# Local attention in a decoder: the output projection of one sequence-layer in one block of 256 tokens instead of two blocks of 128

## Chip, core and metric

The kernel runs on one core of one Trainium2 chip. The metric is the device time of one execution in microseconds (us). The engines of the core work side by side: TensorE (PE for its matmuls, PEld for its weight loads), VectorE (DVE), ScalarE (ACT), GpSimd (POOL) and SyncE (SP), which here only issues DMAs. Each works through its own instructions in order and waits on semaphores of the others.

## What is computed

A decoder of three parts over 8 sequences of 256 tokens with 128 features, all in float32: a state-space block, a cross-attention block and six layers of local attention with a feed-forward. The change lies in the local attention, whose layer the reference writes like this:

```python
def attn_layer(x, Wqkv, qs, ksc, Wo):
    q, k, v = jnp.split(x @ Wqkv, 3, -1)
    sh = lambda t: t.reshape(b, n, HEADS, DIM_HEAD).transpose(0, 2, 1, 3)
    q, k, v = (sh(q), sh(k), sh(v))
    q = l2norm(q) * qs
    k = l2norm(k) * ksc
    ...
    out = local_attention(q, k, v)      # windows of 32, each sees itself and the one before
    out = out.transpose(0, 2, 1, 3).reshape(b, n, INNER)
    return out @ Wo                     # INNER = 16 heads * 64 = 1024, back to 128
for i in range(DEPTH):                  # 6
    x = attn_layer(shift_tokens(x), ...) + x
    x = ffn_layer(shift_tokens(x), ...) + x
```

The last product, `out @ Wo`, and the sum with `x` behind it are what the change touches.

## The kernel before, in words

The first two parts (state-space, cross-attention) end at about 715 us of the profile and are not touched. The third part handles 48 sequence-layers (6 layers of 8 sequences) one after the other. The work is not left to a scheduler on TensorE and VectorE: inside `tc.manual_schedule` their instructions stand in the order in which the program issues them. That order is the list `slots` (lines 1174 to 1201). `run(n)` goes through it once for each sequence-layer n; I call this a **pass**. A slot `(f, k, ...)` does step `f` for sequence-layer n + k, so that one pass works on three neighbouring sequence-layers. A blank line divides the list into four groups, the **tiles** 1 to 4 of a pass. On TensorE they hold:

- tiles 1 and 3: `value` (v_ps, line 875), `scores` (s_ps, line 979), `turn` of the queries (qkT_ps, line 931), a piece of a feed-forward, `turn_weights` (pT_ps, line 1021), `query_key` (qk_ps, line 875);
- tiles 2 and 4: `project_out` (y_ps, line 1052), `attend` (o_ps, line 1038), `turn` of the keys (qkT_ps, line 931), a piece of a feed-forward, `turn_weights`, `query_key`.

The other engines in this part:

- VectorE: for each tile the two rotary products of `query_key` (lines 892 and 893, they read qk_ps), the sums of squares (ss, line 905), maximum and sum of the weights (mx, lines 1000, 1012, 1013). In tiles 1 and 3 also twice `masked` (line 991, reads s_ps), in tiles 2 and 4 also the sum `x + y_ps` of `project_out` (line 1060) and two 32x32-block transposes of o_ps into oT (line 1046).
- ScalarE: the squares of qk_ps (sq, line 898), the copies out of qkT_ps (lines 938 for queries, 941 for keys), of v_ps (918) and pT_ps (1025), roots and exponentials (line 98).
- GpSimd: 896 (rotary sum), 1001 and 1014 (weights), 924 (`normalise`: queries or keys times their inverse length).

Keys that tile 2 turns were normalised in tile 1 of the same pass, one tile before. Those that tile 4 turns, and all queries, were normalised two tiles before or more.

A feed-forward serves a pair of sequences, in pieces spread over two passes by the slots `("ff",)`. In the passes of odd n, tile 2 holds its variance (ln_var, line 1106), behind which ScalarE makes the inverse root (ln_sq, line 98) and VectorE the normalised input (fxn, line 1108), and tile 3 holds its first products (f_ps, line 1122). In the passes of even n the rest follows (lines 1122, 1128, 1150, 1151).

PSUM is handed out from two-buffer pools: "big" tiles of two banks hold qk_ps, v_ps, qkT_ps and two thirds of f_ps; "s" tiles of one bank hold y_ps, pT_ps, ln_var and the like. A matmul into a big tile waits until what was there has been read.

`project_out(n, wh)` (lines 1048 to 1065) does one half of a sequence: eight matmuls accumulate the 1024 inner features in eight blocks of 128, with the weights `Wo` as the stationary operand and 128 tokens of oT as the moving one. In the trace each float32 matmul is two records, so one half is 16 records with 16 weight loads. The half with wh = 0 of sequence-layer n - 1 stands in tile 2 of pass n, the half with wh = 1 in tile 4. `attend(n, 0)` and `attend(n, 1)` fill oT for them: attend(n, 0) in tile 4 of pass n, attend(n, 1) in tile 2 of pass n + 1.

Of the kernel before, what the change touches and what calls it, by code (L numbers as in the profile page):

```python
# [9 lines left out]
FP = mybir.dt.float32  # L10
# [4 lines left out]
P = 128  # L15
# [8 lines left out]
H, HD = 16, 64  # L24
# [25 lines left out]
def decoder_kernel(ctx: ExitStack, tc: tile.TileContext, a: dict, out: bass.AP):  # L50
    nc = tc.nc
    V, A, G, T = nc.vector, nc.scalar, nc.gpsimd, nc.tensor
# [12 lines left out]
    def ps_s(name):  # L65
        return banks[-1].tile([P, 512], FP, tag="s", name=name)
# [4 lines left out]
    def ps_two(name):  # L71

        return banks[-1].tile([P, 2, 512], FP, tag="two", name=name, bufs=1)
# [121 lines left out]
    def new_x(p):  # L195
        return xp.tile([P, TP], FP, tag=f"x{p}", name=f"x{p}")
# [104 lines left out]
    with (  # L301
# [450 lines left out]
        for p in range(NPAIR):  # L752
# [3 lines left out]
            for n in range(NS):  # L756
                state(p, c, n)
                if n == 0:
# [3 lines left out]
                    for h in range(2):  # L762
                        t = ps1.tile([P, TP], FP, tag=f"xm{h}", name="xm_ps", bufs=1)
# [33 lines left out]
    x2 = [None] * NPAIR  # L797
    pools3, fixed3, x3, done = {}, {}, [], set()
    wts, thirds, tabs = {}, {}, {}
# [46 lines left out]
    def batch(xs, b):  # L846
        return xs[b // 2][:, (b % 2) * S : (b % 2 + 1) * S]

    seq = [(d, b) for d in range(DEPTH) for b in range(B)]
    tiles3 = [(wh, g) for wh in range(2) for g in range(2)]  # L850

    got = [{} for _ in seq]

    def shift(n):

        d, b = seq[n]
        if d + 1 < DEPTH:
            if b == 3:
                load(d + 1)
                load_table3(d + 1)  # L860
            if b == 6:
                load_third(d + 1, 0)
        x = batch(x2 if d == 0 else x3, b)
        xs = pools3["a"].tile([P, S], FP, name="xs", bufs=3)
        G.memset(xs[HD:, 0:1], 0.0)
        A.copy(xs[:HD, :], x[:HD, :])
        A.copy(xs[HD:, 1:], x[HD:, : S - 1])
        got[n]["xs"] = xs
        got[n]["ss"] = pools3["a"].tile([P, 4, H], FP, name="ss", bufs=3)
        got[n]["rn"] = pools3["a"].tile([P, 4, H], FP, name="rn", bufs=3)  # L870
# [157 lines left out]
    def attend(n, wh):  # L1028

        o_ps = ps_two("o3_ps")  # L1030
        for g in range(2):
            pT, vz = got[n]["pT", 2 * wh + g], got[n]["vz", 2 * wh + g]
            for j in range(4):
                for i in range(4):
                    for e in range(2):
                        r = slice(e * HD, (e + 1) * HD)
                        c = (4 * g + j) * HD
                        T.matmul(  # L1038
                            o_ps[i * W : (i + 1) * W, e, c : c + HD],
                            lhsT=pT[r, j, i * W : (i + 1) * W], rhs=vz[r, j, i, :],  # L1040
                            start=True, stop=True, tile_position=(e * HD, i * W),
                        )

        oT = got[n]["oT", wh] = pools3["b"].tile([P, 2, 2, 4 * HD], FP, name="oT3")
        for g in range(2):
            V.transpose(oT[:, g], o_ps[:, :, g * 256 : (g + 1) * 256])  # L1046

    def project_out(n, wh):
        d, b = seq[n]
        y_ps = ps_s("y3_ps")  # L1050
        for hb in range(NHB):
            T.matmul(  # L1052
                y_ps[:, :P], lhsT=wts[d][0][:, hb, :],
                rhs=got[n]["oT", wh][:, hb // 4, (hb // 2) % 2, :].rearrange(
                    "p (w h q) -> p h w q", w=4, h=2
                )[:, hb % 2],
                start=(hb == 0), stop=(hb == NHB - 1),
            )
        half = slice(wh * P, (wh + 1) * P)
        V.tensor_tensor(  # L1060
            batch(x3, b)[:, half], batch(x2 if d == 0 else x3, b)[:, half], y_ps[:, :P],
            ALU.add,
        )
        if wh:
            got[n].clear()

    def feed_forward(d, p, b=None):
# [86 lines left out]
    def finish(p, b=None):  # L1154

        at = slice(0, TP) if b is None else slice(b * S, (b + 1) * S)
        x = x3[p][:, at]
        m = at.stop - at.start
        V.tensor_tensor(x, x, x2[p][:, at], ALU.add)
        yield from layernorm_steps(x, x)  # L1160
        yield
        tp = ps_s("st_ps")[:, :m]
        for j in range(m // P):
            T.transpose(tp[:, j * P : (j + 1) * P], x[:, j * P : (j + 1) * P], ident)
        ot = pools3["w"].tile([P, INNER], FP, tag="wqkv", name="st_o", bufs=4)[:, :m]
        A.copy(ot, tp)
        o = out[2 * p : 2 * p + 2] if b is None else out[2 * p + b : 2 * p + b + 1]
        nc.sync.dma_start(
            out=o.rearrange("b (c q) d -> q (b c) d", q=P),
            in_=ot.rearrange("q (c d) -> q c d", d=D),  # L1170
        )
        yield
# [4 lines left out]
    q, k = 0, 1  # L1177
# [4 lines left out]
        (peak, 0, 2), ("end", 1), ("ff",), (turn_weights, 0, 0), (add_weights, 0, 1),  # L1182
        (query_key, 1, k, 1), (root, 1, k, 0), (normalise, 1, k, 0),

        ("end", 1), (weigh, 0, 2), (place, 0, 2), (project_out, -1, 0),
        (attend, -1, 1), (squares, 1, k, 1), (turn, 1, k, 0),
        (peak, 0, 3), ("end", 0), ("ff",), (turn_weights, 0, 1), (add_weights, 0, 2),
        (query_key, 2, q, 0), (root, 1, k, 1), (normalise, 1, k, 1), (shift, 3),
# [3 lines left out]
        (peak, 1, 0), ("end", 1), ("ff",), (turn_weights, 0, 2), (add_weights, 0, 3),  # L1192
        (root, 2, q, 0), ("late",), (query_key, 2, q, 1), (normalise, 2, q, 0),

        (weigh, 1, 0), (place, 1, 0), (project_out, -1, 1),
        (attend, 0, 0), (squares, 2, q, 1), (turn, 1, k, 1),
        (peak, 1, 1), ("end", 0), ("end", 1), ("ff",), (turn_weights, 0, 3), (add_weights, 1, 0),
        (query_key, 2, k, 0), (root, 2, q, 1), (normalise, 2, q, 1),
# [4 lines left out]
    def ends():  # L1203

        while True:
            while queue and next(queue[0], queue) is queue:
                queue.pop(0)
            yield

    end = ends()  # L1210

    def run(n):
        nonlocal ff
        for f, *args in slots:
            k, *args = args or [0]
            if f == "ff" or (f == "late" and n % 2):
                next(ff, None)
            elif f == "late":
                pass
            elif f == "end":  # L1220
                if k != n % 2:
                    next(end)
            elif 0 <= n + k < len(seq) and (f, n + k, *args) not in done:
                f(n + k, *args)
                if f is project_out and args[0]:
                    d, b = seq[n + k]
                    last = d == DEPTH - 1
                    if b % 2:
                        ff = feed_forward(d, b // 2)
                        next(ff)  # L1230
                    elif last and b == B - 2:
                        queue.extend((feed_forward(d, b // 2, 0), finish(b // 2, 0)))
                    if last and b % 2 and b > 1:
                        queue.append(finish(b // 2 - 1))
# [27 lines left out]
    with tc.tile_pool(name="s2", bufs=2, reuse_waits="tile") as sp:  # L1262
# [52 lines left out]
        for p in range(NPAIR):  # L1315
# [6 lines left out]
            oT = sp.tile([P, NHB, TP], FP, name="oT2", bufs=1)  # L1322
# [9 lines left out]
            y_ps = ps_s("y2_ps")  # L1332
            for hb in range(NHB):
                T.matmul(
                    y_ps, lhsT=w2["wo"][:, hb, :], rhs=oT[:, hb, :], start=(hb == 0), stop=(hb == NHB - 1)
# [11 lines left out]
    with ExitStack() as st:  # L1347
        cp = st.enter_context(tc.tile_pool(name="s3c", bufs=1, reuse_waits="tile"))
        pools3["b"] = st.enter_context(tc.tile_pool(name="s3", bufs=2, reuse_waits="tile"))
        fixed3["mask"] = cp.tile([P, NW, 2 * W], FP, name="mask")  # L1350
        nc.sync.dma_start(out=fixed3["mask"], in_=a["c_mask"])


        fixed3["kz"] = cp.tile([P, NHB, W + S], FP, name="kz")
        fixed3["vzs"] = [cp.tile([P, 4, 4, HD], FP, name=f"vz{i}") for i in range(6)]
        for t in [fixed3["kz"]] + fixed3["vzs"]:
            G.memset(t, 0.0)
        x3.extend(new_x(p) for p in range(NPAIR))

        with tc.manual_schedule(engines={mybir.EngineType.PE, mybir.EngineType.DVE}):  # L1360
            shift(1)
            for n in range(-1, len(seq)):
                run(n)
            project_out(len(seq) - 1, 0)
            attend(len(seq) - 1, 1)
            for _ in ff:
                pass
            next(end)
            project_out(len(seq) - 1, 1)
            tail = feed_forward(DEPTH - 1, NPAIR - 1, 1)  # L1370
            queue.append(finish(NPAIR - 2))
            while queue:
                next(tail, None)
                next(end)
            for _ in tail:
                pass
            for _ in finish(NPAIR - 1, 1):
                pass
# [86 lines left out]
```

## Time and profile before

| | us |
|---|---|
| three timed runs | 2239.37, 2244.81, 2244.76 |
| their median | 2244.76 |
| span of the profiled execution, first to last instruction | 2235.6 |
| PE busy in it | 2096.8 (94%) |
| DVE busy | 1743.8 (78%) |
| POOL busy | 1636.2 (73%) |
| ACT busy | 1422.2 (64%) |

The span of the profiled execution leaves out what lies before its first and after its last instruction; the three timed runs are 3.8 to 9.2 us longer. Of the groups of instructions, the projection's are among the costlier ones on TensorE: 1536 matmul records of line 1052 with 187.5 us of busy time, and as many weight loads.

A row of the timeline gives the start of a group, the time from its start to its end, engine, line, operation, the tile written and the tiles read, the number of instructions, and in brackets how long the engine stood idle before it and what ended that. Records of TensorE overlap: the end of a group is later than the start of the next one.

### The profile page before, as it was taken

To read this page: it belongs to the slowest core of one execution; us is meant where nothing else is said; L and a number is where in the kernel's file an instruction comes from. 1 tells how busy PE (TensorE), PEld (TensorE's weight loads), DVE (VectorE), ACT (ScalarE), POOL (GpSimd) and SP (SyncE) were. 2 spreads that over 40 slices of the span, in tenths; PEclk is the share of its full clock that TensorE was granted. 3 is DMA by queue.
4 is the path that set the end of the run, shared out by engine and by line. 5 is a ranking of instruction groups with operands and counts; after the bars stand their busy time and mean duration, and the time that the engine had idled before them with its cause. 6 is when DMAs were issued, how large, how long until landed. Compare 5 with 4: busy or idle time off the path is not lost.

```text
span 2235.6 us, 77068 instructions
## 1 busy us (share of the span) xinstructions
PE 2096.8 (94%) x32482; PEld 1314.8 (59%) x32482; DVE 1743.8 (78%) x2533; ACT 1422.2 (64%) x2432; POOL 1636.2 (73%) x1440
## 2 busy tenths in 40 slices
PE   7787879999998999999999999999999999999986
PEld 3232334444445766666767767676767767676663
DVE  5988986353467988888888888888888888888762
ACT  4544546455556776777767677777767677777554
POOL 3988985132268988888888888888888888888750
PEclk8888889999999999999999999999999999999998
DMA  4434431000204444334443434343443434333330
GB/s 124 119 104 100 105 102 31 1 5 1 83 7 68 71 71 95 67 71 75 74 88 71 79 65 94 68 79 67 75 88 69 78 67 84 68 65 64 65 62 10
DMA packets 438326, 155.41 MB, mean 70 GB/s; under 512 B 401886, under 2 KB 418140, under 8 KB 437852
## 3 DMA queue, kind: packets, MB, share of 16 engines
q1 hardware_dynamic: 437500, 150.10, 34.2%
q8 instruction: 255, 4.18, 0.8%
q14 instruction: 91, 0.75, 0.1%
q10 hardware_dynamic: 480, 0.38, 0.1%
HBM read 54.68 MB, written 1.31 MB: 25 GB/s over the span
## 4 chain that ended last, share of the span: by engine, by line
PE 73%; DVE 13%; ACT 7%; issue 4%; POOL 3%; DMA 0%; SPq 0%; DVEq 0%; POOLq 0%; ACTq 0%
PE qk_ps L875 13%; PE y_ps L1052 8%; PE qkT_ps L931 7%; PE o_ps L1038 7%; PE f_ps L1122 6%; PE v_ps L875 6%; PE s_ps L979 5%; DVE m L691 4%; PE pT_ps L1021 3%; PE f_ps L1150 3%; PE o_ps L1296 2%; PE pr L279 2%; PE s_ps L1277 2%; DVE wz L721 2%; ACT ln_sq L98 1%
## 5 line engine op out<-in xcount | busy, mean ns | idle before, releaser
L896 POOL TENSOR_TENSOR qk<-qk,rb 128x512 f32<-128x512 f32 x384 | 481.0, 1275 | 49.0 <-DVE rb L893 30.6
L924 POOL TENSOR_TENSOR qk<-qk,rn 128x1024 f32<-128x1024 f32 x192 | 365.5, 1904 | 12.8 <-ACT rn L98 12.8
L875 PE MATMUL qk_ps<-wqkv,xs 128*128 128x512 f32 x768 | 363.3, 595 | 2.4 <-ACT kz L941 1.4
L1001 POOL TENSOR_TENSOR pw<-pw,mx 128x512 f32<-128x512 f32 x192 | 202.1, 1052 | 164.6 <-DVE mx L1000 164.3
L898 ACT ACTIVATE sq<-qk_ps 128x1024 f32<-128x1024 f32 x192 | 197.0, 1026 | 165.8 <-PE o_ps L1038 122.6
L892 DVE TENSOR_TENSOR qk<-qk_ps,tab 128x1024 f32<-128x1024 f32 x192 | 228.9, 1192 | 66.6 <-PE qk_ps L875 65.1
L905 DVE TENSOR_REDUCE ss<-sq 128x16 f32<-128x1024 f32 x192 | 229.4, 1195 | 6.2 <-ACT sq L898 6.1
L893 DVE TENSOR_TENSOR rb<-qk_ps,tab 128x1024 f32<-128x1024 f32 x192 | 233.3, 1215 | 0.0
L1014 POOL TENSOR_TENSOR pw<-pw,mx 128x512 f32<-128x512 f32 x192 | 200.4, 1044 | 39.1 <-ACT fxn L1109 32.0
L1286 POOL TENSOR_TENSOR ws<-w 128x512 f32<-128x512 f32 x64 | 81.4, 1272 | 196.8 <-ACT w L98 154.1
L1052 PEld LDWEIGHTS y_ps<-oT,wo 128*128 128x128 f32 x1536 | 186.2, 192 | 46.6 <-issue 33.5
L931 PE MATMUL qkT_ps<-ident,qk 128*128 128x128 f32 x1536 | 210.6, 280 | 2.9 <-POOL qk L924 2.9
L1052 PE MATMUL y_ps<-oT,wo 128*128 128x128 f32 x1536 | 187.5, 275 | 1.9 <-ACT pT L1025 1.6
L1046 DVE STREAM_TRANSPOSE oT<-o_ps 128x512 f32<-128x512 f32 x192 | 126.1, 695 | 80.9 <-PE o_ps L1038 80.9
L875 PEld LDWEIGHTS qk_ps<-wqkv,xs 128*128 128x128 f32 x768 | 131.2, 191 | 97.2 <-issue 92.7
L979 PEld LDWEIGHTS s_ps<-kz,qT 64*32 64x32 f32 x12288 | 138.2, 105 | 74.5 <-issue 33.4
L875 PE MATMUL v_ps<-wqkv,xs 128*128 128x512 f32 x384 | 180.5, 592 | 0.3 <-ACT sq L898 0.3
L931 PEld LDWEIGHTS qkT_ps<-ident,qk 128*128 128x128 f32 x1536 | 165.9, 141 | 23.0 <-POOL qk L924 3.8
L98 ACT ACTIVATE ab<-dt,aa 128x512 f32<-128x512 f32 x128 | 87.6, 689 | 143.1 <-DVE m L691 142.9
L726 POOL TENSOR_TENSOR dw<-wz 128x512 f32<-128x512 f32 x128 | 133.9, 1046 | 56.1 <-DVE wz L721 56.1
L691 DVE TENSOR_TENSOR_SCAN m<-dw,ab 128x256 f32<-128x256 f32 x256 | 160.9, 669 | 12.8 <-POOL mc L693 11.4
L1038 PE MATMUL o_ps<-vz,pT 64*32 64x64 f32 x12288 | 168.0, 225 | 1.7 <-issue 1.7
(217 smaller groups left out, 4178.7 us busy)
## 6 DMA issues: line engine op xcount, KB each, us to landing
vz<-v SPq DMA_DIRECT2D x1152, 64.0 KB, 2.2
rows<-bc_dram SPq DMA_DIRECT2D x126, 256.0 KB, 3.9
vz<-v SPq DMA_DIRECT2D x576, 32.0 KB, 2.1
wqkv<-in_L_ffn_Wqkv SPq DMA_DIRECT2D x18, 512.0 KB, 4.4
wo<-in_L_ffn_Wo SPq DMA_DIRECT2D x48, 64.0 KB, 2.6
w<-in_L_ffn_W SPq DMA_DIRECT2D x6, 341.0 KB, 3.1
t_in<-in_x SPq DMA_DIRECT2D x4, 256.0 KB, 3.4
wkv<-in_L_xattn_Wkv SPq DMA_DIRECT2D x1, 1024.0 KB, 7.9
```

The source lines that it names most:

```text
L691: V.tensor_tensor_scan(m[:, t], i["dw"][:, t], i["ab"][:, t], 0.0, ALU.add, ALU.mult)
L875: T.matmul(pr[:, i * 512 : (i + 1) * 512], lhsT=got[n]["xs"][:, tb * P : (tb + 1) * P], rhs=thirds[seq[n][0], c][:, i * 512 : (i + 1) * 51 ...
L892: V.tensor_tensor(t, p3, cs, ALU.mult)
L893: V.tensor_tensor(rb, p3, sn, ALU.mult)
L896: G.tensor_tensor(t[:, :, o], t[:, :, o], rb[:, :, f], ALU.add)
L905: V.tensor_reduce(got[n]["ss"][:, 2 * c + tb, :], got[n]["sq"], AX.X, ALU.add)
L924: G.tensor_tensor(t, t, r, ALU.mult)
L931: T.transpose(t_ps[:, hb * P : (hb + 1) * P], t[:, 2 * hb : 2 * hb + 2, :].rearrange("p h d -> p (h d)"), ident,)
L979: T.matmul(s_ps[i * W : (i + 1) * W, e, c : c + 2 * W], lhsT=qT[r, 4 * g + i, j * W : (j + 1) * W], rhs=kz[r, 4 * g + i, k0 : k0 + 2 * W], ...
L1001: G.tensor_tensor(pw, pw, mx[:, 0].unsqueeze(3).to_broadcast([P, 4, 2, 2 * W]), ALU.subtract)
L1038: T.matmul(o_ps[i * W : (i + 1) * W, e, c : c + HD], lhsT=pT[r, j, i * W : (i + 1) * W], rhs=vz[r, j, i, :], start=True, stop=True, tile_p ...
L1052: T.matmul(y_ps[:, :P], lhsT=wts[d][0][:, hb, :], rhs=got[n]["oT", wh][:, hb // 4, (hb // 2) % 2, :].rearrange("p (w h q) -> p h w q", w=4 ...
```

## The change

Both halves are projected at once, in tile 4, and nothing is projected in tile 2. For this oT of both halves is one tile (of one buffer, twice as large as each of the two before); the matmuls take 256 tokens each, eight instead of two times eight for a sequence-layer; one sum of 256 columns takes the place of two of 128. The last sequence-layer keeps its two halves.

```diff
-        oT = got[n]["oT", wh] = pools3["b"].tile([P, 2, 2, 4 * HD], FP, name="oT3")
+        if "oT" not in got[n]:
+            got[n]["oT"] = pools3["b"].tile([P, 2, 2, 2, 4 * HD], FP, name="oT3", bufs=1)
         for g in range(2):
-            V.transpose(oT[:, g], o_ps[:, :, g * 256 : (g + 1) * 256])
+            V.transpose(got[n]["oT"][:, wh, g], o_ps[:, :, g * 256 : (g + 1) * 256])

-    def project_out(n, wh):
+    def project_out(n, whs=(0, 1)):
         d, b = seq[n]
+        m = len(whs) * P
         y_ps = ps_s("y3_ps")
+        oT = got[n]["oT"][:, whs[0] : whs[-1] + 1]
         for hb in range(NHB):
             T.matmul(
-                y_ps[:, :P], lhsT=wts[d][0][:, hb, :],
-                rhs=got[n]["oT", wh][:, hb // 4, (hb // 2) % 2, :].rearrange(
-                    "p (w h q) -> p h w q", w=4, h=2
-                )[:, hb % 2],
+                y_ps[:, :m], lhsT=wts[d][0][:, hb, :],
+                rhs=oT[:, :, hb // 4, (hb // 2) % 2, :].rearrange(
+                    "p t (w h q) -> p t h w q", w=4, h=2
+                )[:, :, hb % 2],
                 start=(hb == 0), stop=(hb == NHB - 1),
             )
...
-        ("end", 1), (weigh, 0, 2), (place, 0, 2), (project_out, -1, 0),
+        ("end", 1), (weigh, 0, 2), (place, 0, 2),
         (attend, -1, 1), (squares, 1, k, 1), (turn, 1, k, 0),
...
-        (weigh, 1, 0), (place, 1, 0), (project_out, -1, 1),
+        (weigh, 1, 0), (place, 1, 0), (project_out, -1),
         (attend, 0, 0), (squares, 2, q, 1), (turn, 1, k, 1),
...
-            project_out(len(seq) - 1, 0)
+            project_out(len(seq) - 1, (0,))
             attend(len(seq) - 1, 1)
...
-            project_out(len(seq) - 1, 1)
+            project_out(len(seq) - 1, (1,))
```

In the built programs the orders of ScalarE, GpSimd and SyncE are the same before and after; on TensorE and VectorE only the projection's own instructions move.

More of the change, by code (lines that the diff above doesn't have):

```diff
@@ L1042, in attend @@
                         )
-        oT = got[n]["oT", wh] = pools3["b"].tile([P, 2, 2, 4 * HD], FP, name="oT3")
+        if "oT" not in got[n]:
+            got[n]["oT"] = pools3["b"].tile([P, 2, 2, 2, 4 * HD], FP, name="oT3", bufs=1)
         for g in range(2):
-            V.transpose(oT[:, g], o_ps[:, :, g * 256 : (g + 1) * 256])
-    def project_out(n, wh):
+            V.transpose(got[n]["oT"][:, wh, g], o_ps[:, :, g * 256 : (g + 1) * 256])
+    def project_out(n, whs=(0, 1)):
         d, b = seq[n]
+        m = len(whs) * P
         y_ps = ps_s("y3_ps")
+        oT = got[n]["oT"][:, whs[0] : whs[-1] + 1]
         for hb in range(NHB):
             T.matmul(
-                y_ps[:, :P], lhsT=wts[d][0][:, hb, :],
-                rhs=got[n]["oT", wh][:, hb // 4, (hb // 2) % 2, :].rearrange(
-                    "p (w h q) -> p h w q", w=4, h=2
-                )[:, hb % 2],
+                y_ps[:, :m], lhsT=wts[d][0][:, hb, :],
+                rhs=oT[:, :, hb // 4, (hb // 2) % 2, :].rearrange(
+                    "p t (w h q) -> p t h w q", w=4, h=2
+                )[:, :, hb % 2],
                 start=(hb == 0), stop=(hb == NHB - 1),
             )
-        half = slice(wh * P, (wh + 1) * P)
+        half = slice(whs[0] * P, whs[0] * P + m)
         V.tensor_tensor(
-            batch(x3, b)[:, half], batch(x2 if d == 0 else x3, b)[:, half], y_ps[:, :P],
+            batch(x3, b)[:, half], batch(x2 if d == 0 else x3, b)[:, half], y_ps[:, :m],
             ALU.add,
         )
-        if wh:
+        if whs[-1]:
             got[n].clear()
@@ L1224, in run @@
                 f(n + k, *args)
-                if f is project_out and args[0]:
+                if f is project_out:
                     d, b = seq[n + k]
```

## Prediction

> **What bounds the kernel now.** I read the page first, then the table of waits between 760 and 2180 us, then the timeline of one odd and one even pass. On the page:
>
> ```profile
> PE 2096.8 (94%) x32482; PEld 1314.8 (59%) x32482; DVE 1743.8 (78%) x2533; ACT 1422.2 (64%) x2432; POOL 1636.2 (73%) x1440
> ...
> PE 73%; DVE 13%; ACT 7%; issue 4%; POOL 3%; DMA 0%; SPq 0%; DVEq 0%; POOLq 0%; ACTq 0%
> ```
>
> TensorE is busy 94% of the span and 73% of the chain that ended last. But an average does not say what happens where work is taken out. The table of waits does (engine and line that waited, releaser, total us, times, longest):
>
> ```profile
> DVE oT L1046 <- PE o_ps L1038: 78.0, 91, 1.7
> ...
> PE f_ps L1122 <- ACT sq L898: 13.8, 22, 0.8
> ...
> DVE fxn L1108 <- ACT ln_sq L98: 12.0, 22, 0.7
> ```
>
> TensorE has one wait that comes back: 22 times, some 0.63 us each, once in every odd pass with a feed-forward, at f_ps in tile 3. At that point the others are late, not TensorE. The timeline of pass 23 shows what they are late with (tile 2 begins at 1407.01, tile 3 at 1414.54, tile 4 at 1424.57):
>
> ```profile
> 1407.01 1.95 PE L1052 MATMUL y_ps<-oT,wo 128*128 128x128 f32 x16
> ...
> 1407.68 1.90 POOL L924 TENSOR_TENSOR qk<-qk,rn 128x1024 f32<-128x1024 f32 x1
> ...
> 1408.77 1.21 DVE L893 TENSOR_TENSOR rb<-qk_ps,tab 128x1024 f32<-128x1024 f32 x1
> 1408.88 1.78 PE L1038 MATMUL o_ps<-vz,pT 64*32 64x64 f32 x128
> ...
> 1410.08 1.03 ACT L898 ACTIVATE sq<-qk_ps 128x1024 f32<-128x1024 f32 x1 [1.69 <-DVE rb L893]
> 1410.60 1.09 PE L931 MATMUL qkT_ps<-ident,qk 128*128 128x128 f32 x8
> ...
> 1410.89 1.31 DVE L1046 STREAM_TRANSPOSE oT<-o_ps 128x512 f32<-128x512 f32 x2 [0.72 <-PE o_ps L1038]
> ...
> 1411.72 1.01 ACT L941 COPY kz<-qkT_ps 128x1024 f32<-128x1024 f32 x1 [0.62 <-PE qkT_ps L931]
> ...
> 1414.37 1.21 DVE L1108 SCALAR_TENSOR_TENSOR fxn<-ln_xc,cols,ln_sq 128x512 f32<-128x512 f32 x1 [0.46 <-ACT ln_sq L98]
> ...
> 1418.66 1.02 ACT L898 ACTIVATE sq<-qk_ps 128x1024 f32<-128x1024 f32 x1 [0.44 <-DVE rb L893]
> ...
> 1419.74 2.84 PE L1122 MATMUL f_ps<-fxn,w 128*128 128x512 f32 x6 [0.78 <-ACT sq L898]
> ```
>
> f_ps needs the big PSUM tile that holds qk_ps of tile 2, free once ScalarE has squared it (1418.66 to 1419.68). That square waits for VectorE, which goes without a gap from fxn at 1414.37 over mx, the reciprocal and the rotary products. **So between the removed block and the added one stands a point that VectorE and ScalarE set.**
>
> **The change, part by part.**
>
> The price of a block. From one record's start to the next: y_ps (1.95 - 0.275)/15 = 0.112 us, 0.275 being the mean record of line 1052 on the page. For 256 columns this even pass has a row with the same weights' size:
>
> ```profile
> 1444.76 1.46 PE L1150 MATMUL f_ps<-fh,w 128*128 128x256 f32 x6
> ```
>
> (1.46 - 0.38)/5 = 0.216 us, 0.38 being the mean record of that group. Sixteen records of 128 columns take 1.79 us, sixteen of 256 take 3.46. So tile 2 loses 1.79, tile 4 gains 3.46 - 1.79 = 1.67, and TensorE's own work shrinks by 0.12 us a pass, 47 x 0.12 = 5.6 us in all. Eight weight loads of 192 ns go too, but they lie beside the matmuls and set nothing. The new operand is read in pieces of 32 columns, as the old one was; from the side of the rows, a record could cost between half of qk_ps's 512 columns (in pass 23 four records last 1.88, one 0.595 on the page: (1.88 - 0.595)/3 = 0.428, half of it 0.214) and twice the old one (0.223), which is no saving at all. I take 0.216, a row of just this width.
>
> A page has this differently. By the Trainium skill ("TensorE: Matmul & The Clock Gate", section "Back-to-back issue gap") a stream of pairs of weight load and matmul was measured at about 81 ns a matmul for 128 columns and 131 ns for 512, which makes width nearly free. An estimate from it for 256 columns is 98 ns, the saving then 32 x 81 - 16 x 98 ns = 1.0 us a pass, some 48 us for 47 passes. The rows above (0.112, 0.216, 0.429 us) follow the columns; I go by them.
>
> VectorE: two sums of 0.28 us become one of 256 columns; the nearest row, ln_xc of line 1102 with 128x256, has 0.41. In tile 4 it ends before o_ps is ready, for which VectorE waits there anyway (0.94 us in pass 23), so it is free; in tile 2 0.19 us of VectorE go. If that cover were gone, it would cost 0.13 us a pass. The single buffer of oT adds no wait: attend's transposes in tile 4 stand behind the projection that reads it, on TensorE's own order. ScalarE, GpSimd and SP keep their order; nothing of theirs is moved past anything.
>
> An **odd pass** after the change, with pass 23's times. TensorE reaches o_ps 1.79 us earlier. Its next block, qkT at 1410.60, needs the keys from GpSimd (line 924), done at 1407.68 + 1.90 = 1409.58, and that chain started from s_ps of tile 1, which has not moved. So qkT gains only some 0.95. VectorE ends rb at 1409.98 and can go on with the transposes at once: it gains its wait of 0.72 and the 0.19 of the sum. ScalarE starts sq at 1410.08 as before, right behind rb; its next instruction follows 0.92 us later (1418.66 to the one at 1419.58), so the copy of the keys starts at 1411.00 instead of 1411.72. Behind it stand, without a gap, the root of the variance and the copy of pT, so ln_sq is ready 0.72 earlier; VectorE, which would be ready for fxn before that, starts it 0.72 earlier; all that follows to f_ps moves by the same 0.72. **Of the 1.79 us taken out, f_ps keeps 0.72: exactly the wait that VectorE had at o_ps.** TensorE stands idle for the rest, at qkT and, longer than now, at f_ps. Then tile 4 adds 1.67, and o_ps there starts 0.95 later than before. In tile 4 TensorE is ahead of no one: VectorE waits 2.40 us for its qk_ps in this pass, so nothing gives the 0.95 back.
>
> Over the 22 odd passes from 3 to 45, the wait of VectorE before the transposes of tile 2 in their timelines is 0.39 to 1.15 us, sum 12.3, mean 0.56. An odd pass costs 1.67 - 0.56 = 1.11; 22 x 1.11 = +24.4 us.
>
> An **even pass**: the keys are done 2.1 to 3.1 us before qkT of tile 2 in all of them (2.38 in pass 24), more than the 1.79; VectorE ends rb 1.16 us before the transposes; tile 3 has no wait of TensorE. The whole 1.79 is kept, and the pass gains 0.12; 21 x 0.12 = -2.5 us.
>
> The **four others**: passes 1 and 2 have no feed-forward; the keys are 0.69 and 0.51 us early, so they gain about 0.6 and 0.45 and lose 1.67: +2.3. Pass 46 is like an even one (-0.1), in pass 47 TensorE waits for others in most tiles; I take +1.0, between nothing and 1.67. Together +3.2.
>
> **Sum:** 24.4 - 2.5 + 3.2 = +25 us on a span of 2235.6, so 2261. The timed runs are 3.8 to 9.2 us longer than that span; on their median of 2244.76 it makes **2270 us**, slower by 1.1%.
>
> **Rivals.**
>
> *TensorE keeps what it saves* (not slower). If the wait at f_ps is not set by the square but by something that TensorE itself releases, both blocks cancel and only 47 x 0.12 = 5.6 us go: 2239. For it: TensorE is 94% busy, and a wait's releaser is inferred. Against it: the wait comes 22 times at the same place, each time as the square ends. It decides from the point at which f_ps of an odd pass comes 1.67 us earlier than now; VectorE's idle time from tile 2 to there, with the sum's 0.19, is 0.56 + 0.55 (12.0/22 at fxn) + 0.19 = 1.30 in the mean, which is not enough.
>
> *Even passes lose as well.* Should a wait in tile 2 or 3 hold them as it holds odd ones, 21 x (1.11 + 0.12) = 26 us come on top: 2296. Their margin at qkT is only 0.3 to 0.5 us in most. Against it: VectorE has over 1 us of idle time there before o_ps and again before s_ps.
>
> *The change does not narrow TensorE's work*: at 0.223 us a record the 5.6 us do not go: 2276, inside the range.
>
> **How the numbers follow.** Forecast 0.80, TensorE keeps it 0.15, even passes lose too 0.05. Inside the forecast: if odd passes keep nothing of the 1.79, +12.3, and if a record of 256 columns takes 0.223 besides, +5.6, so up to 2288; if VectorE gives back all of its idle time (1.30 for 0.56), -16.3, so 2254, and with the fastest of the three runs as the base (5.4 lower) 2249. That range leaves out 0.20. About 0.3% is what a measurement of this kernel can tell from no change, 6.7 us. The second case gives 0.09 within it and 0.06 faster; all else is slower, 0.85.
>
> **What would show it.** The wait of f_ps for the square grows from 13.8 us, to about 1.0 us in pass 23; a new wait of qkT (line 931) for GpSimd's keys (line 924) of 0.7 to 0.95 us in odd passes; the wait of the transposes at o_ps vanishes in tile 2 of odd passes; from one tile 2 to the next, odd passes last 34.2 instead of 33.1 us and even ones 29.5 instead of 29.6; y_ps has 784 records, 0.216 us apart. Wrong would make it: f_ps of odd passes early by over 1.3 us, or records of y_ps far below 0.216.

## The result, and the profile after

| | before | after |
|---|---|---|
| median of four timed runs | 2242.15 (2239.37 to 2244.81) | 2260.86 (2257.83 to 2265.09) |
| span of the profiled execution | 2235.6 | 2261.8 |

The changed kernel is slower: 1.0089 of the time before, 95% interval 1.0069 to 1.0108, or 15 to 24 us. The profiled execution of after took 2263.66 us by its own time. The two spans differ by 26.2 us, somewhat more than the timed runs.

In the changed kernel the lines behind line 1041 stand up to 3 higher: the projection's matmul is 1055, its sum 1063, the transposes 1047, fxn 1111 and its first products f_ps 1125. The page after, first the busy times, then the shares of the chain that ended last, then the projection's group (count, busy us and mean ns of one, idle before):

```profile
PE 2092.3 (93%) x31730; PEld 1274.2 (56%) x31730; DVE 1742.2 (77%) x2486; ACT 1422.5 (63%) x2432; POOL 1635.0 (72%) x1440
...
PE 65%; DVE 20%; ACT 8%; issue 3%; POOL 3%; DMA 1%; SPq 0%; ACTq 0%; DVEq 0%; POOLq 0%
...
L1055 PE MATMUL y_ps<-oT,wo 128*128 128x256 f32 (+1 forms) x784 | 174.3, 375 | 1.6 <-ACT pT L1025 1.4
```

TensorE issues 752 records fewer, is busy 4.5 us less, and the kernel is 26 us longer. The chain says where: TensorE's share fell from 73% to 65%, VectorE's rose from 13% to 20%. The table of TensorE's waits of after, from 760 to 2200 us (engine and line that waited, releaser, total us, times, longest):

```profile
PE f_ps L1125 <- ACT sq L898: 21.1, 21, 1.1
PE qkT_ps L931 <- POOL qk L924: 17.1, 22, 1.0
```

The wait at f_ps grew from 13.8 to 21.1 us, and one that was not there, for the keys from GpSimd, has 17.1: together 24.4 us of new waiting, beside a span that is 26.2 us longer. Both come once in each odd pass. Pass 23 of after, in its timeline:

```profile
1422.72 1.09 PE L931 MATMUL qkT_ps<-ident,qk 128*128 128x128 f32 x8 [0.94 <-POOL qk L924]
1422.98 1.30 DVE L1047 STREAM_TRANSPOSE oT<-o_ps 128x512 f32<-128x512 f32 x2
...
1424.08 1.01 ACT L941 COPY kz<-qkT_ps 128x1024 f32<-128x1024 f32 x1
...
1426.38 1.05 POOL L1001 TENSOR_TENSOR pw<-pw,mx 128x512 f32<-128x512 f32 x1
1426.71 1.27 DVE L1111 SCALAR_TENSOR_TENSOR fxn<-ln_xc,cols,ln_sq 128x512 f32<-128x512 f32 x1 [0.68 <-ACT ln_sq L98]
...
1432.14 2.84 PE L1125 MATMUL f_ps<-fxn,w 128*128 128x512 f32 x6 [1.03 <-ACT sq L898]
1436.98 3.62 PE L1055 MATMUL y_ps<-oT,wo 128*128 128x256 f32 x16
...
1440.53 1.68 PE L1038 MATMUL o_ps<-vz,pT 64*32 64x64 f32 x128
1440.63 0.42 DVE L1063 TENSOR_TENSOR x<-x,y_ps 128x256 f32<-128x256 f32 x1 [1.10 <-PE y_ps L1055]
1442.33 1.31 DVE L1047 STREAM_TRANSPOSE oT<-o_ps 128x512 f32<-128x512 f32 x2 [1.27 <-PE o_ps L1038]
```

Tile 2 begins at 1419.99 here, with attend. The reader is to see four things: TensorE waits 0.94 us for the keys; the transposes of tile 2 no longer wait for o_ps; f_ps waits 1.03 us for the square; and from y_ps in tile 4 to the next o_ps are 3.55 us, where one half had 1.87.

To see what an odd pass keeps, I took the median start of TensorE's groups in the odd passes 5 to 43, counted from the attend of tile 4 of the pass before (t2 and t4 are tiles):

```
             o_ps t2   qkT t2   f_ps t3   y_ps t4   o_ps t4
before        13.85    15.57    24.62     29.46     31.33
after         12.13    14.76    24.20     29.04     32.58
difference    -1.72    -0.81    -0.42     -0.42     +1.25
```

Of the 1.72 us by which o_ps comes earlier, 0.81 are left at qkT and 0.42 at f_ps; then the longer block adds 1.67. These are differences between medians; taken pass by pass, f_ps of the odd passes 3 to 45 comes 0.53 us earlier in the mean, and 1.67 - 0.53 = 1.14. In length, from the attend of one tile 4 to the next, the odd passes 3 to 45 lose 1.14 us in the mean against before (25.0 in all), the even ones 4 to 44 gain 0.13 (2.75 in all); passes 1, 2 and 46 lose 1.16, 1.38 and 0.51, all behind them 0.17 (pass 47 loses 1.33 and what follows it gains 1.17), and 0.78 lie ahead of the part that was changed.

### The profile page after: what moved, and what is told of

It reads as the page before. It is cut to its first block, busy times and chain, and to the rows that moved or that the text cites. A ratio compares the mean times of both kernels' runs of the same rounds, so it can differ in the third digit from the quotient of the medians.

```text
span 2261.8 us, 75535 instructions
## 1 busy us (share of the span) xinstructions
PE 2092.3 (93%) x31730; PEld 1274.2 (56%) x31730; DVE 1742.2 (77%) x2486; ACT 1422.5 (63%) x2432; POOL 1635.0 (72%) x1440
## 4 chain that ended last, share of the span: by engine, by line
PE 65%; DVE 20%; ACT 8%; issue 3%; POOL 3%; DMA 1%; SPq 0%; ACTq 0%; DVEq 0%; POOLq 0%
PE qk_ps L875 11%; PE y_ps L1055 7%; PE f_ps L1125 6%; PE v_ps L875 5%; PE qkT_ps L931 5%; PE o_ps L1038 5%; PE s_ps L979 5%; DVE m L691 4%; PE pT_ps L1021 3%; PE f_ps L1153 3%; DVE rb L893 2%; PE o_ps L1299 2%; DVE qk L892 2%; PE pr L279 2%; ACT sq L898 2%
## 5 line engine op out<-in xcount | busy, mean ns | idle before, releaser
L1001 POOL TENSOR_TENSOR pw<-pw,mx 128x512 f32<-128x512 f32 x192 | 202.5, 1055 | 201.7 <-DVE mx L1000 201.2
L1038 PEld LDWEIGHTS o_ps<-vz,pT 64*32 64x32 f32 x12288 | 151.1, 105 | 52.7 <-issue 35.6
L98 ACT ACTIVATE pw<-pw 128x512 f32<-128x512 f32 x192 | 120.9, 630 | 88.4 <-POOL pw L1001 88.3
L1055 PE MATMUL y_ps<-oT,wo 128*128 128x256 f32 (+1 forms) x784 | 174.3, 375 | 1.6 <-ACT pT L1025 1.4
```

Source lines behind the costliest of these rows:

```text
L1038: T.matmul(o_ps[i * W : (i + 1) * W, e, c : c + HD], lhsT=pT[r, j, i * W : (i + 1) * W], rhs=vz[r, j, i, :], start=True, stop=True, tile_p ...
L1055: T.matmul(y_ps[:, :m], lhsT=wts[d][0][:, hb, :], rhs=oT[:, :, hb // 4, (hb // 2) % 2, :].rearrange("p t (w h q) -> p t h w q", w=4, h=2)[ ...
```

## Experiments

The theory after the result: tile 4 pays 1.67 us in every pass, and odd passes can't keep the 1.79 of tile 2, because two points between the tiles come at a time that TensorE does not set: the keys at qkT (GpSimd) and the square ahead of f_ps (the chain of VectorE and ScalarE). Rivals: only one of the two points matters; or the longer block costs odd passes something by itself. All kernels but the repeated one were timed in turn with before on the same chip; its median there was 2240.3 to 2241.55 us.

**The kernel before once more**, for what two profiles of one kernel differ by.

> The kernel before once more, for a second profile: how far the length of odd and even passes and the whole span differ between two profiles of the same kernel. Expected: passes equal within 0.1 us in the mean.

Span 2235.3 against 2235.6; odd passes +0.05, even ones -0.01 us in the mean. Differences of a tenth of a microsecond a pass can be read.

**Both halves in tile 4, still of 128 columns.** The place alone, without the width.

```diff
-        ("end", 1), (weigh, 0, 2), (place, 0, 2), (project_out, -1, 0),
+        ("end", 1), (weigh, 0, 2), (place, 0, 2),
...
-        (weigh, 1, 0), (place, 1, 0), (project_out, -1, 1),
+        (weigh, 1, 0), (place, 1, 0), (project_out, -1, 0), (project_out, -1, 1),
```

> The move alone, without the width: both halves are projected in tile 4, one after the other, with 128 tokens each. My theory (a fixed point at f_ps between tile 2 and tile 4, set by VectorE and ScalarE): the move is what costs. Tile 4 gains 1.79 us instead of 1.67, so odd passes lose 1.23 instead of 1.11 and even passes 0.0: some 47 x 0.12 = 5.6 us more than the changed kernel, about 25 us over the kernel before. Rival (the wide block is what costs): about the time of the kernel before.

2287.66 us, 1.0209 of before [1.0194, 1.0224]: 47 us slower, nearly twice what was expected. Up to y_ps of tile 4 odd passes stand as in after (o_ps 12.08, qkT 14.76, f_ps 24.19, y_ps 29.03), so the place alone brings both waits. But their o_ps of tile 4 comes at 33.27, not 32.58. TensorE's waits in this kernel:

```profile
PE f_ps L1122 <- ACT sq L898: 21.3, 21, 1.1
PE qkT_ps L931 <- POOL qk L924: 18.4, 22, 1.2
PE y_ps L1052 <- ACT fg L1139: 7.0, 22, 0.3
```

and in its timeline tile 4 of pass 22 and of pass 23, TensorE's rows of the projection and attend:

```profile
1413.30 3.73 PE L1052 MATMUL y_ps<-oT,wo 128*128 128x128 f32 x32
1416.96 1.68 PE L1038 MATMUL o_ps<-vz,pT 64*32 64x64 f32 x128
...
1446.61 1.95 PE L1052 MATMUL y_ps<-oT,wo 128*128 128x128 f32 x16
1448.87 2.05 PE L1052 MATMUL y_ps<-oT,wo 128*128 128x128 f32 x16 [0.32 <-ACT fg L1139]
1450.85 1.68 PE L1038 MATMUL o_ps<-vz,pT 64*32 64x64 f32 x128
```

The first block is the even kind: 32 records without a gap, 3.66 us to o_ps. The second is the odd kind, with a new wait in its middle, 4.24 us: the second half's y_ps needs the other one-bank PSUM tile, which a piece of the feed-forward's first products holds until ScalarE's gelu has read it. So the width is worth more than its 0.12 us a pass: one y_ps tile in place of two also saves odd passes 0.58 (4.24 - 3.66). Against after, odd passes take 14.6 us more in all and even ones 2.1; another 7.8 lie behind pass 46, where two groups of TensorE stand still in their middle for 1.87 and 2.30 us without a releaser in the trace. What those are I leave open.

**The block of tile 2 taken out, nothing put in tile 4.** What is kept of 1.79 us when nothing is added.

```diff
+        if not wh and n + 1 < len(seq):
+            V.tensor_scalar(batch(x3, b)[:, :P], batch(x2 if d == 0 else x3, b)[:, :P], 1.0, None, ALU.mult)
+            return
```

> One half of the change alone: the block of tile 2 is left out and nothing is added in tile 4. The projection of the first 128 tokens is not computed (only copied through). My theory: odd passes with a feed-forward keep only VectorE's wait at o_ps, 0.56 us in the mean, even passes the whole 1.79: 22 x 0.56 + 21 x 1.79 + some 3 for the four others = 53 us less than before. Rival (TensorE keeps what is taken from it): 47 x 1.79 = 84 us less.

2192.52 us, 0.9793 [0.9776, 0.981], 48 us less (theory 53, rival 84). Even passes gain 1.83 us, all that was taken out. Odd passes gain 0.20. Of the theory's 0.56 a part went to the experiment itself: the copy that stands in for the sum takes VectorE 0.77 us (the sum had 0.28), and fxn became longer, 1.62 us against 1.12. TensorE's waits in this kernel:

```profile
PE f_ps L1127 <- ACT sq L898: 26.7, 22, 1.3
PE qkT_ps L931 <- POOL qk L924: 19.0, 22, 1.3
```

With that the rival, TensorE keeping what it saves, is out: nine tenths of a removed block vanish in odd passes.

**After, without the keys' wait.** In tile 1 the first 128 tokens' keys are left unnormalised.

```diff
+        if (c, tb) == (1, 0):
+            return
```

> The changed kernel, but the keys of the first 128 tokens are not normalised on GpSimd, so that qkT of tile 2 does not wait for that. My theory: the wait of some 0.8 us at qkT goes in odd passes and comes back at f_ps, whose square is set by VectorE and ScalarE; odd passes stay 1.1 us longer than before, and the time is that of the changed kernel within 0.3%. Rival (the late keys are the price): odd passes get the 0.8 back, some 17 us less than the changed kernel, near the kernel before.

2255.47 us, 1.0066 [1.0051, 1.0081]. The wait at qkT for GpSimd is gone, the one at f_ps has 23.3 us in 22 times:

```profile
PE f_ps L1127 <- ACT sq L898: 23.3, 22, 1.1
```

qkT of tile 2 now starts at 13.81 (before 15.57, after 14.76), f_ps at 23.88. TensorE runs ahead by 1.76 and has 0.74 left at f_ps. Odd passes still lose 0.83 against before: taking away the keys' wait alone gives back 0.30 of the 1.14.

**Both kernels without the softmax's maximum, sum and normalising.** This takes VectorE's and GpSimd's load off the chain to f_ps. Before and after, each with:

```diff
-        V.tensor_reduce(mx[:, 0], pw, AX.X, ALU.max)
-        G.tensor_tensor(pw, pw, ..., ALU.subtract)
-        with_table(A.activation, pw, pw, AF.Exp)
+        with_table(A.activation, pw, pw, AF.Exp, scale=0.01)
-        V.tensor_reduce(mx[:, 1], pw, AX.X, ALU.add)
-        V.reciprocal(mx[:, 1], mx[:, 1])
-        G.tensor_tensor(pw, pw, ..., ALU.mult)
-        turned.append(A.copy(..., t_ps))
+        turned.append(A.activation(..., t_ps, AF.Copy, scale=1.0 / 64))
```

> The kernel before with less work on VectorE and GpSimd: the maximum and the sum of the attention weights and the two GpSimd products behind them (lines 1000, 1001, 1012 to 1014) are left out, and the exponential gets a small scale and pT a constant factor so that values stay bounded. It is the base for the next run. Expected: the waits of TensorE at f_ps go (22 x 0.63 = 14 us), so about 2230.

> The same change on that lighter kernel (maximum, sum and normalising of the attention weights left out). My theory: where VectorE and GpSimd are not late, TensorE keeps what it saves; odd passes may wait 0.2 us for the keys, so the change gives between 0 and -6 us against the lighter kernel before. Rival (the longer block in tile 4 is itself what costs): some 20 us slower than the lighter kernel before.

2215.51 (0.9887 of before [0.9874, 0.9901]) and 2234.98 (0.9969 [0.9958, 0.998]). The first is 15 us below what was expected of it: its odd passes gain 0.83 us, more than the 0.63 of their wait at f_ps, and that is 18.3 of the 22.0 us by which its span is shorter. The change still costs 19.5 us: the expectation for the pair fell. The wait at f_ps is gone from both, as meant, yet odd passes lose 0.94 and even ones gain 0.21. The changed one's waits and pass 23:

```profile
PE qkT_ps L931 <- POOL qk L924: 23.9, 22, 1.5
```

```profile
1407.72 1.90 POOL L924 TENSOR_TENSOR qk<-qk,rn 128x1024 f32<-128x1024 f32 x1 [1.37 <-ACT rn L98]
...
1409.68 1.09 PE L931 MATMUL qkT_ps<-ident,qk 128*128 128x128 f32 x8 [1.05 <-POOL qk L924]
```

Now the keys hold all of it. GpSimd, with lines 1001 and 1014 gone, stands idle 1.37 us ahead of line 924 for ScalarE's inverse root, and takes its 1.90 us all the same. So neither point alone is the cause: taking either away leaves 0.83 or 0.94 of 1.14.

**Both points taken away at once**: the two edits above together, in the kernel before and in the changed one.

> The kernel before, without the softmax's maximum, sum and normalising (as in light_before: exp with the scale 0.01, 1/64 on the copy of pT) and also without normalising the keys of the first 128 tokens in tile 1 (as in no_keys): both waits at which TensorE was seen late between tile 2 and f_ps of odd passes are taken away at once. It is the base for free_after. Both theories: like light_before or a few us below it (2205 to 2216 us), since neither wait cost TensorE anything while the two halves stood apart; no wait at f_ps and none at qkT.

> The same two removals made in the changed kernel. Theory (two points hold odd passes, the keys at qkT and the chain of VectorE and ScalarE at f_ps, and each alone keeps 0.8 to 0.95 of the 1.14 us): with both gone TensorE keeps the 1.79 us of tile 2, odd passes differ from free_before by -0.1 like even ones, and the whole by about -5 us (between -8 and +3, if a trace of a wait is left). Rival (the longer block in tile 4 costs odd passes by itself, whatever waits stand before it): odd passes still +0.8 or more, the whole +15 to +20 us. Between the two would lie a third wait that only now shows, at a line other than 931 and f_ps's.

2211.35 (0.9872 [0.9856, 0.9889]) and 2208.81 (0.9859 [0.9845, 0.9874]): the changed one is 2.5 us faster in the medians, 3.6 by the spans (2208.5 and 2204.9), of which passes 1 to 47 hold 0.7. The four runs of each kernel spread over 3.7 and 4.7 us and overlap, so this is no cost rather than a measured gain. qkT of tile 2 comes 1.78 us earlier than in its base (15.59, 13.81), f_ps 1.47 (23.81, 22.34), odd passes lose 0.16 where they lost 1.14, even ones gain 0.18. What odd passes lack to the even ones, 0.34, is the rest of the wait at f_ps, seen at the matmuls and at the weight load ahead of them:

```profile
PEld f_ps L1122 <- ACT sq L898: 7.6, 19, 0.5
...
PE f_ps L1122 <- ACT sq L898: 2.3, 12, 0.2
```

(7.6/22 = 0.35.) The cost of the change thus hangs on the two points and on nothing in the long block itself: where both are absent, the same edit costs nothing that can be measured.

**A filler ahead of f_ps.** If TensorE stands idle at f_ps, work that is ready can be put there: the turn of the weights of tile 3 ahead of the feed-forward's piece, in the kernel before and in the changed one.

```diff
-        (peak, 1, 0), ("end", 1), ("ff",), (turn_weights, 0, 2), (add_weights, 0, 3),
+        (peak, 1, 0), ("end", 1), (turn_weights, 0, 2), ("ff",), (add_weights, 0, 3),
```

> The kernel before, with turn_weights of tile 3 put ahead of the piece of the feed-forward, so that TensorE does pT_ps (0.44 us) while f_ps waits for the square. My theory: f_ps starts when it did, and 0.44 of the 0.63 us of waiting is filled in the 22 odd passes: 9.7 us less (2232), if ScalarE's changed order takes nothing back. Rival (the wait is TensorE's own): no change.

> The changed kernel with the same reordering of tile 3. My theory: its wait at f_ps, 1.0 us in odd passes, is filled by 0.44: 9.7 us less than the changed kernel, still some 10 over the kernel before. Rival: no change against the changed kernel, 20 over the kernel before.

On before 2230.64 us, 0.9953 [0.9941, 0.9966]: 10.9 us faster than before, and faster than both kernels. Odd passes gain 0.44 us. Its waits:

```profile
PE f_ps L1122 <- ACT sq L898: 3.9, 18, 0.3
```

On the changed kernel 2258.3, 1.0078 [1.0064, 1.0092]. Its odd passes gain 0.49 us, the span 9.9 against after's, but the medians differ by only 2.6 (2260.86, from another round of runs). The profiled run is the fastest of five (2253.74). It is 17 us over before, where some 10 had been expected, and 27.7 us over the same edit on before (19.4 by the spans). The profile shows the saving in the odd passes; the timed runs do not settle its size.

**fxn with one of its inputs in PSUM.** In all kernels above in which GpSimd's line 1001 runs beside fxn, fxn ended 0.545 to 0.554 us after that line's end, whether fxn had begun before or after it; it took 0.752 us where GpSimd was idle. In pass 23 of after GpSimd works without a gap from the keys (line 924, 1420.76) to the end of line 1001 (1427.43), so GpSimd would have a hand in the second point too. To see it, the inverse root that fxn multiplies by is left in the PSUM tile of the variance; no instruction is added or moved.

```diff
-        inv_root(sq, var, eps_t)
-        V.scalar_tensor_tensor(xn, xc, col("ff_g", d), sq, ALU.mult, ALU.mult)
+        inv_root(var, var, eps_t)
+        V.scalar_tensor_tensor(xn, xc, col("ff_g", d), var, ALU.mult, ALU.mult)
```

> The kernel before, with the inverse root that fxn multiplies by left in its PSUM tile instead of being written to SBUF; the instructions and their order are the same. Seen in the runs so far: fxn ends 0.545 to 0.55 us after the end of GpSimd's line 1001 whenever that runs beside it (all odd passes of before and after), and lasts 0.752 us where GpSimd is idle. Theory (fxn, with two inputs in SBUF, and GpSimd's operation exclude each other, so that f_ps hangs on GpSimd's subtraction): with one input in SBUF fxn lasts 0.7 to 0.8 us though line 1001 runs beside it, ends some 0.3 to 0.4 us earlier, the wait at f_ps falls from 13.8 us to 3 to 6, and odd passes gain 0.3 to 0.45 us: 7 to 10 us in all. Rival (fxn is long for another reason, or both merely wait for the same thing): fxn stays at 1.1 us and the time within 2 us of before.

> The same in the changed kernel. Theory: fxn 0.7 to 0.8 us instead of 1.28, f_ps 0.5 us earlier, its wait falls from 21.1 us to about 11, odd passes gain 0.5 us on the changed kernel: about 11 us (it then costs some 15 to 18 us over the same edit in the kernel before, since the keys at qkT still keep 0.94 of each odd pass). Rival: 1.28 us as before, no gain.

On before 2233.75 us, 0.9965 [0.9953, 0.9977], 6.9 less; on the changed kernel 2254.54, 1.006 [1.0046, 1.0073], where the change alone had 1.0089. Odd passes gain 0.32 and 0.43 us. The changed one in pass 23:

```profile
1424.56 1.05 POOL L1001 TENSOR_TENSOR pw<-pw,mx 128x512 f32<-128x512 f32 x1
1424.85 0.75 DVE L1111 SCALAR_TENSOR_TENSOR fxn<-ln_xc,cols,ln_var 128x512 f32<-128x512 f32 x1 [0.66 <-ACT ln_var L98]
```

and TensorE's waits in it:

```profile
PE qkT_ps L931 <- POOL qk L924: 17.8, 22, 1.2
PE f_ps L1125 <- ACT sq L898: 12.5, 21, 0.7
```

fxn lasts 0.75 us with line 1001 beside it, and here ends 0.01 us before it. In the mean it is 0.38 us shorter in before and 0.50 in the changed kernel; ScalarE's inverse root, which now writes PSUM, releases it only 0.03 us sooner. The wait at f_ps falls from 21.1 to 12.5 (in before from 13.8 to 6.2), the one at qkT stays. So of the second point about 0.4 us a pass is GpSimd holding up fxn. The change costs as much as ever between these two, 20.8 us in the medians: I had expected 15 to 18, reckoning with a larger gain in the changed kernel than in the other.

## Why the prediction was right, and where it was off

The sign and the mechanism held, and the span did almost to the microsecond (2261 predicted, 2261.8). By the prediction's own steps:

- **Price of a block.** Right. The records of y_ps stand 0.216 us apart, and the one sum has 0.42 us (0.41 predicted). The figures of the Trainium skill weighed there ("TensorE: Matmul & The Clock Gate", section "Back-to-back issue gap"), by which width would be nearly free, do not hold for this kernel's float32 matmuls: 16 records of 256 columns cost 3.55 us up to the next group. Of the weight loads 16 records go from a pass (752 in 47), not the eight that the prediction counts.
- **Odd passes.** Right in size: 1.14 us against 1.11 predicted, 25.0 in all against 24.4. In pass 23, counted from the start of tile 2, qkT came 0.86 us earlier (0.95 predicted), the copy of the keys 0.62 (0.71), fxn 0.64 and f_ps 0.58 (0.72); the two waits were 0.94 (0.7 to 0.95) and 1.03 (about 1.0). Over the odd passes 3 to 45 f_ps came 0.53 us earlier in the mean, beside the 0.56 expected. That these are so close is in part luck. The prediction took as its measure VectorE's wait at o_ps, but VectorE did not use up its idle time: its wait ahead of fxn grew, from 0.53 to 0.68 us in the mean. What moved was ScalarE: the square of tile 2 starts when it did (0.01 us earlier), the copy of the keys behind it 0.65 earlier, now without a wait, and fxn with it 0.66 earlier. ScalarE's wait ahead of that copy happened to have the same mean as VectorE's at o_ps, 0.56 us. fxn, which the prediction took to last as long wherever it starts, then gave 0.13 back: it had to let GpSimd's line 1001 go by, and its median grew from 1.12 to 1.28 us. 0.66 - 0.13 = 0.53.
- **That one point sets it.** Too narrow. The prediction rested the loss on the chain of VectorE and ScalarE, with the keys on the side, and GpSimd had no part in that chain. Either point alone keeps most of the loss, and GpSimd has a part in both. So a repair of only one of them would have been forecast wrongly from the prediction's text, as my own expectation for the lightened pair was.
- **Even passes.** Right: -0.13 against -0.12.
- **The four others.** 3.2 predicted, 1.16 + 1.38 + 0.51 + 0.17 = 3.2 measured, though parted otherwise: pass 46 loses 0.51, where nothing was expected, and pass 47 with what follows it next to nothing, where I took 1.0.
- **From span to time.** This step failed, and it is the 9 us between 2270 and 2260.86. I took the 9.2 us from the span of 2235.6 to the median 2244.76 for something that lies around every execution. The runs show 1.8 to 1.9 us between an execution's time and its own span (2263.66 and 2261.8; 2237.1 and 2235.3). The rest was scatter between runs: before has 2237 to 2245. A part of it lies ahead of what was changed: the first attend begins at 709.3 to 715.0 us in the nine profiles of kernels that do the same up to there. 2261 + 1.9 = 2263 would have been the number.
- **The timed difference.** 18.7 us between the medians, up to 24 within the interval, stands against 26.2 in the profiles. Two of the four runs of after (2263.66 and 2265.09, granted clock 0.968 and 0.967) are 6 us above the other two (2258.05 and 2257.83, at 0.971 and 0.972), and the profiled one is of the upper pair. That is an order of four runs, not a shown cause.
- **Rivals.** TensorE keeping what it saves: out by the kernel that only removes. Even passes losing as well: out by their rows. The width not narrowing the work: out by 0.216, and the two halves in tile 4 show that it is worth more than its columns.

## What to carry to other kernels

Ahead of moving a block on the busiest engine, list the points between the old place and the new at which another engine delivers: what is saved ahead of such a point is waited away there, and what is added behind it is paid in full. Look for the second such point as well, since removing one shows the other. A wait that comes back at one line can be worked on directly: a filler of ready work there gave 0.5%, and an input of one operation moved from SBUF to PSUM 0.35%.

## What had not been expected of the hardware

VectorE's fxn has the same shape in all kernels, and what it took was set by GpSimd's line 1001 beside it. Its rows (duration as min/median/max in ns), first of after, then of the kernel that only removes, then of the changed one with the inverse root in PSUM:

```profile
L1111 DVE SCALAR_TENSOR_TENSOR fxn<-ln_xc,cols,ln_sq x24: 483/1278/1283, 787.7 to 2231.7; 128x512 f32<-128x512 f32 x23, 128x256 f32<-128x256 f32 x1
```

```profile
L1113 DVE SCALAR_TENSOR_TENSOR fxn<-ln_xc,cols,ln_sq x24: 485/1622/1627, 784.7 to 2159.0; 128x512 f32<-128x512 f32 x23, 128x256 f32<-128x256 f32 x1
```

```profile
L1111 DVE SCALAR_TENSOR_TENSOR fxn<-ln_xc,cols,ln_var x24: 481/748/749, 790.6 to 2225.4; 128x512 f32<-128x512 f32 x23, 128x256 f32<-128x256 f32 x1
```

With both tensors in SBUF it ends 0.55 us after GpSimd's operation ends, in each of the seven kernels where the two meet; the earlier it starts, the longer its row. With one tensor in PSUM it takes 0.75 us beside the same operation. The Trainium skill ("SBUF — State Buffer", section "SBUF: two separate sides") says that GpSimd and a VectorE operation with two SBUF inputs hold a shared port pair exclusively, the one that starts first making the other wait. The runs agree, but for who comes first: in the kernel that only removes, the record of line 1001 begins 0.03 us after that of fxn, and fxn waits for it all the same (1.62 us). The start of a record need not be the moment at which an operation takes the ports, so the order of two records this close does not tell which will wait. To start a VectorE operation earlier thus need not end it earlier; a row that grew by half is a sign to look for GpSimd beside it.
